# Where three scatters stand among GpSimd's gathers in a two-layer graph kernel on one core

## The chip, the cores and the metric

The kernel runs on one core of one Trainium2 chip. The metric is the device time of one execution in microseconds (us); smaller is better. A core has TensorE (PE in the profile), VectorE (DVE), ScalarE (ACT), GpSimd (POOL) and SyncE (SP), which run side by side, and 16 DMA engines that all of them feed. Each engine takes its own instructions strictly in program order: an instruction that waits holds up everything behind it on that engine. GpSimd issues here the DMAs whose row numbers are data: gathers (rows of a DRAM tensor into an SBUF tile) and scatters (rows of an SBUF tile into a DRAM tensor). The instruction on GpSimd ends when the transfer is issued; the data land later.

## The reference, cut to what matters

x has 2708 rows of 512 floats, adj is 2708 x 2708, with about 0.3% of its places filled.

```python
rowsum = adj.sum(axis=1)
d = where(rowsum > 0, rowsum ** -0.5, 0)
z = ((d[:, None] * adj * d[None, :]) @ x) @ W + b
h = layernorm(x + relu(z))                            # layer 0
xn = h @ W_node + b_node
feats = einsum('nd,hdf->hnf', xn, K)                  # 4 heads
s = leaky_relu(feats . A_self + feats . A_neigh)
attn = softmax(s[:, :, None] - 1e10 * (1 - adj))      # over the neighbours j
out = layernorm(h + relu(mean over heads of attn @ feats))   # layer 1
```

In layer 1 the term that is multiplied by 1e10 decides the softmax: a row gives all its weight to the neighbour with the largest adj value (s is the same for all j of a row). So layer 1 is a gather. With u = h @ M + c, where M and c join W_node, b_node and the mean of K, row i of the result is layernorm(h[i] + relu(u[top(i)])).

## The kernel before, in words

Rows go in blocks of 128: 21 full blocks (NS = 21) and one of 20 rows. A preparation finds the entries of each adj row and makes v = d * (x @ W), which goes to DRAM as v_d. **Layer 0** is a loop over the 21 blocks and, in each, over 9 chunks (C = 9); a step is n = 9 * block + chunk. A chunk is one gather of 128 rows of v_d on GpSimd (`fetch`, L650) and one product that adds them up (a matmul, L713, or an operation on VectorE, L703). Rows that do not fit this scheme, the last 20 among them, are "listed": at most 128 rows that are computed densely as an extra block L = 21.

When a block's sum is complete, `norm_1` (L754 and L755) and the steps behind it make h. A table `agenda` holds what is to be done at which step; `after(n, b, args)` enters the steps of block b: centre (L768), root, normalise, turn h (L244), `u_product` (L255) and `u_store` (L861 makes the tile ut from the product, then it is stored). The rows of u go to two DRAM tensors: u_e for the first 18 blocks (EARLY = 18) and u_d for blocks 18, 19 and 20. Blocks 0 to 16 are stored in plain order by SyncE; blocks 17 to 20 and the listed rows by scatters on GpSimd (`put`, L1198), because rows that are listed have to be left out.

**Layer 1.** For each block n a gather `y_fetch(n)` (L1221, called y0 to y20 here) takes the rows u[top(i)] out of u_e into a buffer. Rows whose neighbour lies in u_d are outside the bounds and left alone; they are late rows. `y_1` adds and sums (L1232 on VectorE, then the mean at L773, and the squares on ScalarE, L774), `root_1` and `root_2` make the scale for a group of blocks, `y_3` normalises (L805 on ScalarE or L810 on VectorE), and `out_store` (L1245, SyncE) stores a group. These steps are cut into 34 pieces; piece k holds y_fetch(k) and y_1(k-6). From step 173 to 185 of layer 0, ten pieces are run beside the last two blocks (three steps in four). What is left is run after the loop.

The late rows are packed into four tiles of 128 (NLATE = 4), numbers L+1 to L+4, beside the listed tile L. Each of the four needs its rows of h (`late_h`, a gather from h_d, L650) and its rows of u (a gather from u_d with the index top_d). Tile L has two gathers into one and the same buffer: from u_e with the index top_l (called yL here), and from u_d with top_d; so the second waits until the first has landed. The order of the gathers from u_d is L+1, L+2, L, L+3, L+4 (L1465), and all of them follow every scatter into u_d. Then come y_1, roots and y_3 of the five tiles (L1484 to L1500, in the groups L+1, L+2, L and L+3, L+4), and five scatters into the output (`rows_out`, L1476), which also have to follow the plain stores of the output.

All these buffers come from `row_space` (L656), a ring over two pools of 12 tiles: a tile's space is used again by the 24th request after it.

In the code before, the scatter of block 18 (S18 here) stands at step 180, that of block 19 (S19) at L1445, and that of block 20 (S20) at L1459, all inside `u_store` at L869.

Of the kernel before, what the change touches and what calls it, by code (L numbers as in the profile page):

```python
# [47 lines left out]
P = 128  # L48
# [5 lines left out]
EARLY = 18  # L54
NLATE = 4
# [8 lines left out]
def tile_two_graph_layers(  # L64
# [12 lines left out]
    N, D = x.shape  # L77
# [7 lines left out]
    NS = N // P  # L85
    GROUPS = [0, 4, 12, NB]

    def rows(ib):
        return min(P, N - ib * P)
# [15 lines left out]
    def many(dram_t, lo, hi):  # L105

        return dram_t[lo * P : hi * P, :].rearrange("(n p) d -> p n d", p=P)
# [12 lines left out]
    u_e = dram.tile([EARLY * P, D], F32, name="u_e")  # L120
    u_d = dram.tile([N - EARLY * P, D], F32, name="u_d")
# [534 lines left out]
    def row_space():  # L656

        ring[0] += 1
        if late is not None and ring[0] % 2:
            return late.tile([P, D], F32, name="g2", bufs=12)  # L660
        return g_pool.tile([P, D], F32, name="g", bufs=12)
# [100 lines left out]
    def centred(n, pr, t, junk):  # L762

        s = slice(n, n + 1)
        if n < ROOTS_AT:
            spread(n, pr, t, junk)
        else:
            nc.scalar.activation(junk[:pr], t[:pr], AF.Square, bias=nms[:pr, s], accum_out=sqs[:pr, s])  # L768
# [14 lines left out]
    def norm_2(lo, hi):  # L783

        s = slice(lo, hi)
        nc.gpsimd.tensor_tensor(rss[:, s], sqs[:, s], half_neg[:, : hi - lo], op=ALU.pow)

    def root_1(lo, hi):

        s = slice(lo, hi)  # L790
        nc.scalar.activation(sds[:, s], sqs[:, s], AF.Sqrt, scale=1.0 / D, bias=eps_1)
        nc.vector.tensor_scalar(vrs[:, s], sqs[:, s], 1.0 / D, EPS, op0=ALU.mult, op1=ALU.add)

    def root_2(lo, hi):

        s = slice(lo, hi)
        nc.vector.reciprocal(rss[:, s], sds[:, s])
        nc.vector.tensor_mul(vrs[:, s], vrs[:, s], rss[:, s])
        nc.vector.scalar_tensor_tensor(vrs[:, s], vrs[:, s], -0.5, rss[:, s], op0=ALU.mult, op1=ALU.mult)
        nc.vector.scalar_tensor_tensor(rss[:, s], vrs[:, s], 1.5, rss[:, s], op0=ALU.add, op1=ALU.mult)  # L800
        if hi - lo > 1:
            nc.vector.tensor_mul(nbs[:, s], nms[:, s], rss[:, s])
# [22 lines left out]
    def store_h(done):  # L825

        if done in H_ENDS:
            lo = ([0] + H_ENDS)[H_ENDS.index(done)]
            nc.sync.dma_start(out=many(h_d, lo, done), in_=h_part(lo, done))
# [3 lines left out]
    def turn_h(ib):  # L833
        hTs[ib] = turn(space(ib), P if ib == L else rows(ib), nc.scalar.copy)
# [3 lines left out]
    def u_product(ib):  # L838
        pr = P if ib == L else rows(ib)
        on_pe = searching[0]  # L840
        products_u[ib] = times(hTs.pop(ib), pr, m_sb, c_3 if on_pe else None), on_pe
# [3 lines left out]
    def u_store(ib):  # L845

        pr = P if ib == L else rows(ib)
        if ib == L:
            ut = dl["u"]
        else:  # L850
            if ib >= EARLY - 1:
                ut = row_space()
            else:
                if not ib % 2:
                    u_pair[:] = [pool2.tile([P, 2, D], F32, name="ut", bufs=1)]
                ut = u_pair[0][:, ib % 2, :]
        po, on_pe = products_u.pop(ib)
        if on_pe:
            nc.scalar.copy(ut[:pr], po[:pr])
        else:  # L860
            nc.vector.tensor_add(ut[:pr], po[:pr], c_bc[:pr])  # L861
        if ib < EARLY - 1:
            if ib % 2 or ib == EARLY - 2:
                lo = ib - ib % 2
                nc.sync.dma_start(out=many(u_e, lo, ib + 1), in_=u_pair[0][:, : ib + 1 - lo])
        elif ib == EARLY - 1:
            put(ut, u_e[:, :], dl["own"][:, ib : ib + 1], EARLY * P)
        elif ib != L:
            put(ut, u_d[:, :], dl["own_d"][:, ib : ib + 1], N - EARLY * P)  # L869


    L = NS
    dl = {}
# [7 lines left out]
    def at(n, f):  # L881
        agenda.setdefault(n, []).append(f)
# [314 lines left out]
    def put(t, dst, rows_at, n=N):  # L1197
        nc.gpsimd.indirect_dma_start(  # L1198
            out=dst,
            out_offset=bass.IndirectOffsetOnAxis(ap=rows_at, axis=0),  # L1200
            in_=t,
            in_offset=None,
            bounds_check=n - 1,
            oob_is_err=False,
        )


    ys = {}
    y_fetched = set()

    def y_fetch(n):

        if n in y_fetched:
            return
        y_fetched.add(n)
        ys[n] = row_space()
        fetch_some(ys[n], idx[:, n : n + 1], u_e[:, :], EARLY * P)

    def fetch_some(t, at, src, n):

        nc.gpsimd.indirect_dma_start(  # L1221
            out=t,
            out_offset=None,
            in_=src,
            in_offset=bass.IndirectOffsetOnAxis(ap=at, axis=0),
            bounds_check=n - 1,
            oob_is_err=False,
        )
# [30 lines left out]
    def pieces_y(k):  # L1259
        for _ in range(k):  # L1260
            for f in early_y.pop(0) if early_y else ():
                f()

    def y_ahead(k):

        nexts = [n for n in range(NS) if n not in y_fetched][:k]
        for n in nexts:
            y_fetch(n)

    def late_h(k):  # L1270
        h_of[L + 1 + k] = row_space()
        fetch(h_of[L + 1 + k], P, dl["read"][:, k : k + 1], h_d[:, :])
# [4 lines left out]
    C = len(CHUNKS)  # L1277
# [57 lines left out]
    def normed(b):  # L1335
        k = slice(b, b + 1)
        nc.scalar.activation(nbs[:, k], nms[:, k], AF.Copy, scale=rss[:, k])  # L1337
        norm_3(b, P, space(b))
        store_h(b + 1)

    def after(n, b, args):

        e = max(0, min(7, 15 - b))
        s = -1 if b == EARLY - 1 else 0
        at(n + 1 + s + min(2, e), lambda: centred(*args))
        if b >= ROOTS_AT:
            at(n + 2 + s + min(3, e), lambda: root_1(b, b + 1))
        at(n + 3 + s + min(4, e), lambda: norm_2(b, b + 1) if b < ROOTS_AT else root_2(b, b + 1))
        at(n + 3 + s + min(6, e), lambda: normed(b))
        if b < NS - 1:  # L1350
            at(n + 5 + s + e, lambda: turn_h(b))
            at(n + 7 + s + e, lambda: u_product(b))
        if b < NS - 2:
            at(n + 9 + s + e, lambda: u_store(b))

    def after_listed(n):
        at(n + 2, listed_norm)
        at(n + 3, lambda: root_1(L, L + 1))
        at(n + 5, lambda: root_2(L, L + 1))
        at(n + 5, lambda: norm_v(L, P, h_of[L]))  # L1360
        at(n + 6, lambda: turn_h(L))
        at(n + 8, lambda: u_product(L))
        at(n + 10, lambda: u_store(L))
# [6 lines left out]
    for ib in range(NS):  # L1370
        pr = rows(ib)
        for c in range(C):
            n = ib * C + c
# [60 lines left out]
        if ib < NS - 1:  # L1434
            after(n + 1, ib, args)
# [4 lines left out]
    ib = NS - 1  # L1440
    centred(*args)
    for n in sorted(agenda):
        for f in agenda.pop(n):
            f()
    u_store(ib - 1)  # L1445
    y_ahead(3)
    root_1(ib, ib + 1)
    pieces_y(1)
    root_2(ib, ib + 1)
# [3 lines left out]
    turn_h(ib)  # L1453
    pieces_y(1)
    u_product(ib)
    y_ahead(4)
    pieces_y(3)
    y_ahead(NS)
    u_store(ib)  # L1459
    for k in range(NLATE):  # L1460
        late_h(k)
    ys[L] = row_space()
    fetch_some(ys[L], dl["top"][:, NLATE:], u_e[:, :], EARLY * P)

    order = [L + 1, L + 2, L] + list(range(L + 3, L + 1 + NLATE))  # L1465
    for n in order:
# [180 lines left out]
```

## Time and profile before

| | us |
|---|---|
| median of 5 runs | 504.63 |
| the five runs | 504.63, 507.56, 501.21, 501.43, 506.9 |
| the profiled execution | 502.18 |
| its span, first to last instruction | 500.5 |

| engine | busy, us | share of the span |
|---|---|---|
| PE | 383.3 | 77% |
| DVE | 370.5 | 74% |
| ACT | 318.9 | 64% |
| POOL | 299.1 | 60% |

A row of the timeline gives the start in us from the start of the span, the length in us, the engine, the line of the kernel (L...), the operation, output <- inputs, and in square brackets how long the engine had been idle and what released it. "issue" means that it waited for nothing that the profile shows. A row of the view of waits gives the engine and line that waited, what it waited for, the total in us, how often, and the longest. A row of the view by stretches gives the busy time of PE, PEld (weight load), DVE, ACT and POOL with the number of instructions, the granted clock, the DMA engines' share and GB/s.

### The profile page before, as it was taken

The page shows a single profiled execution, that of the slowest core. Times are in us where ns is not written, and L with a number is a line of the kernel's source. Part 1 is how long each engine was busy: PE and PEld are TensorE (multiplying, and loading weights), DVE is VectorE, ACT ScalarE, POOL GpSimd, SP SyncE. Part 2 cuts the span into 40 slices and gives each one's busy share as a digit, 9 for nine tenths or more (in the row PEclk, how much of TensorE's full clock was granted, in tenths as well). Part 3 has the DMA queues.
Part 4 walks back from the last instruction along what each step waited for, and adds up shares of the span by engine and source line. Part 5 has one row for each costly group of instructions (what it writes and reads, how often), then busy time and mean ns, then how long its engine had stood idle before and what let it go on. Part 6 is the DMA issues. An engine that isn't in the chain of part 4 may idle for free. (4 is left out here: it accounts for less than half of the span.)

```text
span 500.5 us, 5439 instructions
## 1 busy us (share of the span) xinstructions
PE 383.3 (77%) x1299; PEld 176.5 (35%) x1299; DVE 370.5 (74%) x1058; ACT 318.9 (64%) x592; POOL 299.1 (60%) x423
## 2 busy tenths in 40 slices
PE   4978776869959999999867999959997768792000
PEld 3433333434214433333433444524442333351000
DVE  3699989699598899999597689744665375548751
ACT  1699999797972777879764764725662121337851
POOL 2333643453577677777787778776555627647624
PEclk8999999998998999999896999998999799988555
DMA  7999999997578587887999989997959635548972
GB/s 233 424 395 420 402 341 369 372 331 277 179 231 318 171 272 215 295 295 225 303 304 344 346 299 316 371 411 242 333 159 361 183 96 174 191 121 254 313 274 81
DMA packets 50251, 140.66 MB, mean 281 GB/s; under 512 B 9305, under 2 KB 9305, under 8 KB 47376
## 3 DMA queue, kind: packets, MB, share of 16 engines
q0 software_dynamic: 21696, 68.29, 42.8%
q1 hardware_dynamic: 28516, 71.95, 38.6%
q8 instruction: 12, 0.20, 0.2%
q14 instruction: 27, 0.22, 0.1%
HBM read 117.33 MB, written 24.99 MB: 284 GB/s over the span
## 5 line engine op out<-in xcount | busy, mean ns | idle before, releaser
L650 POOL DMA_INDIRECT g<-v_d,l_col x126 | 127.8, 1015 | 61.3 <-issue 30.7
L713 PE MATMUL acc<-g,s 128*128 128x512 f32 x272 | 140.6, 637 | 5.5 <-DMA g<-v_d,l_col 3.4
L255 PE MATMUL acc<-w_sb,sT 128*128 128x512 f32 (+1 forms) x176 | 84.7, 626 | 0.0
L255 PE MATMUL po<-m_sb,sT 128*128 128x512 f32 x176 | 82.8, 615 | 0.7 <-ACT sT L246 0.7
L650 POOL DMA_INDIRECT g<-v_d,cols x63 | 64.8, 1029 | 21.4 <-issue 11.7
L336 DVE MAX8 vals<-a 128x8 f32<-128x896 f32 (+2 forms) x66 | 71.7, 1086 | 4.1 <-ACT a L314 4.1
L337 DVE FIND_INDEX8 ats<-vals,a 128x8 uint32<-128x896 f32 (+2 forms) x66 | 72.0, 1091 | 0.0
L713 PEld LDWEIGHTS acc<-g,s 128*128 128x128 f32 x272 | 49.8, 199 | 53.6 <-issue 45.9
L314 ACT ACTIVATE a<-a 128x2708 f32<-128x2708 f32 (+1 forms) x22 | 54.6, 2480 | 10.5 <-POOL a L329 10.4
L321 ACT ACTIVATE a<-a 128x2708 f32<-128x2708 f32 (+1 forms) x22 | 54.1, 2461 | 3.4 <-DVE ats L337 3.4
L255 PEld LDWEIGHTS po<-m_sb,sT 128*128 128x128 f32 x176 | 34.8, 201 | 45.6 <-issue 40.7
L690 ACT ACTIVATE s<-s,l_val,l_minus 128x128 f32<-128x128 f32 x92 | 45.3, 493 | 3.1
L255 PEld LDWEIGHTS acc<-w_sb,sT 128*128 128x128 f32 (+1 forms) x176 | 33.2, 199 | 35.6 <-issue 35.6
L329 POOL TENSOR_SCALAR_AFFINE_SELECT a<-a 128x128 f32<-128x128 f32 (+1 forms) x22 | 6.3, 286 | 64.7 <-DMA a<-in_adj_dram 63.0
L246 ACT COPY sT<-tp 128x512 f32<-128x512 f32 (+1 forms) x44 | 25.5, 580 | 27.9 <-PE tp L244 27.8
L754 DVE TENSOR_TENSOR vs<-acc,vs 128x512 f32<-128x512 f32 x20 | 13.7, 687 | 35.5 <-PE acc L713 34.5
L703 DVE SCALAR_TENSOR_TENSOR vs<-g,scaled,vs 128x512 f32<-128x512 f32 x53 | 39.4, 744 | 0.5 <-DMA g<-v_d,l_col 0.4
L244 PE MATMUL tp<-ident,x 128*128 128x128 f32 (+1 forms) x88 | 15.0, 297 | 27.8 <-DMA x<-in_x_dram 17.1
L689 ACT ACTIVATE s<-place,l_row 128x128 f32<-128x128 f32 x92 | 35.7, 388 | 0.2 <-PE acc L713 0.2
L1337 ACT ACTIVATE nbs<-nms,rss 128x1 f32<-128x1 f32 x20 | 5.9, 293 | 46.8 <-DVE rss L800 30.2
L768 ACT ACTIVATE xr<-h_late,nms 128x512 f32<-128x512 f32 x13 | 9.3, 715 | 33.0 <-DVE nms L759 33.0
L1221 POOL DMA_INDIRECT g<-u_e,idx x21 | 22.2, 1056 | 7.4 <-issue 4.6
(284 smaller groups left out, 581.4 us busy)
## 6 DMA issues: line engine op xcount, KB each, us to landing
a<-in_adj_dram SPq DMA_DIRECT2D x21, 1354.0 KB, 18.1
x<-in_x_dram SPq DMA_DIRECT2D x21, 256.0 KB, 7.9
l_v<-v_d SPq DMA_DIRECT2D x7, 768.0 KB, 6.4
vs<-v_d SPq DMA_DIRECT2D x10, 512.0 KB, 10.9
xr<-in_x_dram SPq DMA_DIRECT2D x10, 512.0 KB, 9.7
u_e<-ut SPq DMA_DIRECT2D x8, 512.0 KB, 4.9
h_early<-in_L_gnn_K_dram POOLq DMA_DIRECT2D x3, 1024.0 KB, 19.2
v_d<-vs POOLq DMA_DIRECT2D x5, 512.0 KB, 9.8
```

Source lines behind the costliest of these rows:

```text
L246: copy(sT[:, :, :pr], ps[:, :, :pr])
L255: nc.tensor.matmul(po[:pr], sT[:, f, :pr], wt[:, f, :], start=(f == 0 and row_3 is None), stop=(f == ND - 1))
L314: nc.scalar.activation(blocks_a[ib][:pr], blocks_a[ib][:pr], AF.Copy, accum_out=sums[:pr, ib : ib + 1])
L321: nc.scalar.activation(blocks_a[ib][:pr], blocks_a[ib][:pr], AF.Relu, scale=-1.0, accum_out=bad[:pr, NB + ib : NB + ib + 1])
L336: nc.vector.max(out=vals[:pr, ib, t, :], in_=part)
L337: nc.vector.max_index(out=ats[:pr, ib, t, :], in_max=vals[:pr, ib, t, :], in_values=part)
L650: nc.gpsimd.indirect_dma_start(out=t[:pr], out_offset=None, in_=src, in_offset=bass.IndirectOffsetOnAxis(ap=ap, axis=0))
L689: nc.scalar.activation(s[:, :pr], place[:, :pr], AF.Abs, bias=minus_row[:, t : t + 1])
L690: nc.scalar.activation(s[:, :pr], s[:, :pr], AF.Relu, scale=minus_val[:, t : t + 1], bias=val[:, t : t + 1])
L703: nc.vector.scalar_tensor_tensor(vs, g, scaled[:, ib, CHUNKS[c][1], 0:1], vs, op0=ALU.mult, op1=ALU.add)
L713: nc.tensor.matmul(acc[ib][:pr], ss.pop((ib, c))[:k, :pr], g[:k], start=(first and not bias_on_pe(ib)), stop=(c == len(CHUNKS) - 1),)
L1221: nc.gpsimd.indirect_dma_start(out=t, out_offset=None, in_=src, in_offset=bass.IndirectOffsetOnAxis(ap=at, axis=0), bounds_check=n - 1, oo ...
```

## The change

`u_store` no longer scatters blocks 18 to 20; it makes the tile and returns it, and a new function `put_late` scatters it at another place. S18 moves from step 180 to step 188, the loop's last, S19 from ahead of the gathers that follow the loop to behind four of them, and S20 to behind yL, which moves from behind the four gathers of `late_h` to ahead of S20. No instruction is added or taken away; what is computed is the same.

```diff
@@ u_store
         elif ib != L:
-            put(ut, u_d[:, :], dl["own_d"][:, ib : ib + 1], N - EARLY * P)
+            return ut
@@ after
+    kept = []
...
-        if b < NS - 2:
+        if b < EARLY:
             at(n + 9 + s + e, lambda: u_store(b))
+        elif b < NS - 2:
+            at(n + 9, lambda: kept.append((b, u_store(b))))
+            at(NS * C - 1, lambda: put_late(*kept.pop(0)))
+
+    def put_late(ib, ut):
+        put(ut, u_d[:, :], dl["own_d"][:, ib : ib + 1], N - EARLY * P)
@@ behind the loop
-    u_store(ib - 1)
-    y_ahead(3)
+    kept.append((ib - 1, u_store(ib - 1)))
+    y_ahead(4)
+    put_late(*kept.pop())
     root_1(ib, ib + 1)
     pieces_y(1)
...
     u_product(ib)
-    y_ahead(4)
     pieces_y(3)
     y_ahead(NS)
-    u_store(ib)
+    ys[L] = row_space()
+    fetch_some(ys[L], dl["top"][:, NLATE:], u_e[:, :], EARLY * P)
+    put_late(ib, u_store(ib))
     for k in range(NLATE):
         late_h(k)
-    ys[L] = row_space()
-    fetch_some(ys[L], dl["top"][:, NLATE:], u_e[:, :], EARLY * P)
```

## The prediction

> **What bounds the kernel now.** I read the page first. No engine is busy through the span (PE 77%, DVE 74%), and the chain of work that ended last names one instruction of the program's end, so it carries nothing. The change touches only what GpSimd does behind step 180, so I read the timeline from 425 us on, GpSimd first:
>
> ```profile
> 430.56 1.01 POOL L1221 DMA_INDIRECT g<-u_e,idx  x1 [0.30 <-issue]
> 433.84 1.21 POOL L1198 DMA_INDIRECT u_d<-g,own_d  x1 [2.28 <-DVE g L861]
> ...
> 440.85 1.00 POOL L1221 DMA_INDIRECT g<-u_e,idx  x1 [0.31 <-issue]
> 447.44 1.01 POOL L1198 DMA_INDIRECT u_d<-g,own_d  x1 [5.59 <-DVE g L861]
> ...
> 462.59 1.00 POOL L1221 DMA_INDIRECT g<-u_e,idx  x1 [0.30 <-ACT h_early L805]
> 463.89 1.02 POOL L1198 DMA_INDIRECT u_d<-g,own_d  x1 [0.30 <-DVE vrs L799]
> 465.22 1.22 POOL L650 DMA_INDIRECT g<-h_d,to_read  x1 [0.31 <-issue]
> ...
> 470.50 1.00 POOL L1221 DMA_INDIRECT g<-u_e,top_l  x1 [0.30 <-ACT h_late L805]
> 471.81 1.00 POOL L1221 DMA_INDIRECT g<-u_d,top_d  x1 [0.31 <-issue]
> 473.11 1.00 POOL L1221 DMA_INDIRECT g<-u_d,top_d  x1 [0.30 <-ACT g L774]
> 477.76 0.99 POOL L1221 DMA_INDIRECT g<-u_d,top_d  x1 [3.65 <-DMA g<-u_e,top_l]
> ...
> 480.35 1.00 POOL L1221 DMA_INDIRECT g<-u_d,top_d  x1 [0.30 <-issue]
> 488.21 1.01 POOL L1198 DMA_INDIRECT out_dram<-g,to_put  x1 [6.86 <-ACT g L805]
> ```
>
> S18, S19 and S20 are the three rows u_d<-g,own_d. In front of S18 and S19 GpSimd stands still for 2.28 and 5.59 us, because ut is not made yet (DVE L861), with gathers behind it that need nothing of it. In front of S20 there is no wait: it is its place behind y20 that makes it late. And at 477.76 the second gather of tile L stands 3.65 us until yL, issued at 470.50, has landed in the same buffer. Then the waits of VectorE and the rows of VectorE and ScalarE in the same stretch:
>
> ```profile
> DVE vs L754 <- PE acc L713: 10.8, 2, 5.7
> DVE rss L797 <- ACT sds L791: 4.7, 8, 0.9
> DVE l_h L1232 <- DMA g<-u_d,top_d: 3.5, 1, 3.5
> ```
> ```profile
> 476.96 1.52 ACT L805 ACTIVATE h_late<-h_late,nbs,rss 128x512 f32<-128x512 f32 x2 [0.32 <-DVE nbs L802]
> 478.23 0.69 DVE L1232 SCALAR_TENSOR_TENSOR g<-g,g 128x512 f32<-128x512 f32 x1 [0.84 <-DMA g<-u_d,top_d]
> 479.04 0.74 DVE L1232 SCALAR_TENSOR_TENSOR g<-g,g 128x512 f32<-128x512 f32 x1
> 483.48 0.69 DVE L1232 SCALAR_TENSOR_TENSOR l_h<-g,l_h 128x512 f32<-128x512 f32 x1 [3.51 <-DMA g<-u_d,top_d]
> 484.40 0.72 ACT L774 ACTIVATE g<-l_h,nms 128x512 f32<-128x512 f32 x1 [3.58 <-DVE nms L773]
> 485.25 0.30 ACT L791 ACTIVATE sds<-sqs,eps 128x3 f32<-128x3 f32 x1
> ```
> ```profile
> 464.00:478.50 14.50, 0.19 (x2) 0.11 (x2) 10.50 (x46) 12.88 (x27) 8.72 (x9) 0.50 0.93 324
> 478.50:488.20 9.70, 0.00 (x0) 0.00 (x0) 5.00 (x22) 4.64 (x11) 2.24 (x3) 0.50 0.63 242
> ```
>
> No gather y0 to y20 appears among VectorE's waits: the blocks' layer 1 is paced by ScalarE and VectorE in turn (ScalarE busy 12.88 of 14.50 us) and is over at 478.48. From there the end hangs on DMA: VectorE waits 0.84 us for L+1's rows and 3.51 us for L's, issued at 477.76 and used at 483.48 (5.72 us). The roots of the first three tiles need L's squares (end 485.22), the output scatters need the roots, and from 488.21 on all is fixed: five scatters, then 12.3 us to the end.
>
> **The change part by part.** Counted from the loop (a piece at steps 173, 175, 176, 177, 179, 180, 181, 183, 184 and 185), S18 comes to stand behind 10 gathers, S19 behind 14, S20 behind 22 with yL; before, the trace shows 5, 10 and 21. One gather more or less ahead of S18 or S19 would be 1.3 us on GpSimd and change nothing below.
>
> A gather costs GpSimd 1.06 us (mean of the 21 y) and 0.30 us of issue: 1.36 us; a scatter 1.3, a late_h 1.31 (mean 1.01 and 0.30).
>
> *S18.* y5 starts at 431.9 in place of 435.36, since y4 ends at 431.57. Five gathers take 6.8 us, to 438.7; S18, whose tile is made at 433.56, goes there until 440.0. The wait of 2.28 us is gone. The buffers of y5 to y9 were those of block 19's chunks 1 to 5, all multiplied before 430.6 (block 19's sum is read at 430.69), so no wait takes its place.
>
> *S19.* y10 to y13 run from 440.0 to 445.4; their buffers are those of chunks that ended by 433. S19 still waits for its tile (L861 at 446.48 plus 0.68), so it starts at 447.44 as now, its wait about 2 us. Behind it stand y14 to y20, seven in place of eleven: 448.75 to 458.3 (7 x 1.36). y20's buffer is that of block 20's last chunk, read by 444.94.
>
> *yL and S20.* yL goes 458.3 to 459.6 in place of 470.50. S20, its tile made at 455.74 and so no wait, goes to 460.9, 1.7 us sooner than now (463.89 to 459.6) in spite of the gather put ahead of it. Four late_h run to 466.1; the last store of h_d was issued at 449.65, 11 us ahead of them. Then L+1 at 466.1, L+2 at 467.4, L at 468.7, L+3 at 470.0 and L+4 at 471.3. yL needs 7.0 us from its start (470.50 to 477.46); it has landed at 465.3, 3.4 us before L wants its buffer. S20's landing (3.2 us) is over at 462.8.
>
> *What it is worth.* With 5.7 to 7.0 us of landing, L+1 is there by 473.1, L by 475.7, L+4 by 478.3. They are asked for at 477.4 and later, when VectorE has done the last L810 (476.84 + 0.54). So the end goes by engines: L1232 of the three at 477.39, 478.20 and 479.01 (pitch 0.81), the means ready at 478.27, 479.08 and 479.89 (0.88 from a start, as at 478.23 to 479.11), ScalarE free at 478.48, the three squares of 0.87 us (0.72 and 0.19 overlapping) at 478.48, 479.37 and 480.25, the last over at 481.12 in place of 485.22. What follows keeps its order and lengths: a gain of 4.1 us, first output scatter at 484.1. Nothing else on PE, VectorE or ScalarE is moved. Alone, the swap of yL with S20 gives most of it: without the earlier y's, L would go at 474.4 and land at 480.1 in place of 483.48, 3.4 us. The moves of S18 and S19 give the last 0.7 and the reserve.
>
> *DMA.* y5 to y13 move into 431 to 447, where the DMA engines are 53% busy (425 to 447.5), out of a stretch with 71%; the rest moves ahead of 478, out of the stretch with the output stores. I take nothing for it. Bounds: below, the output scatters must follow the last plain store, issued at 478.50; transfers ceased at 485.0 in this execution, so if that stays the scatter goes at 485.0 in place of 488.21 and the gain is 3.2. I take 4.1, since three gathers of 256 KB (0.77 MB, 1.9 us at the 400 GB/s of those microseconds) leave the stretch. Above, 4.4 us is all that ScalarE idles (0.67, 0.14 and 3.58) in this execution.
>
> The Trainium skill (DMA: Bandwidth & Descriptors, Anatomy of one DMA) puts a DMA from GpSimd at about 2.0 us plus its bytes at 436 GB/s, an estimate of 2.6 us for 256 KB. By it yL would have landed at 474.1, there would be almost no wait at 477.76 and the change would be worth under 1 us; the trace shows 7.0 and 5.7 us, and the measurement decides.
>
> The sum: 500.5 - 4.1 = 496.4 us of span; the execution's own time 502.18 - 4.1 = 498.1. The median of the five runs lies 2.45 us over this execution, so from it the sum is 500.5. Two runs lie near 501.3, three at 504.6 to 507.6, so I do not know which kind will be in the middle and take the mean of both, 499.3.
>
> **The rivals.**
>
> *More.* The wait removed is a chain of two landings, 7.0 and 5.7 us. In an execution whose landings are 20% longer the chain grows by 2.5 us and the removed wait with it: 6.6 us, 495.6 from the profiled execution and 498.0 from the median. For it: three runs are 2.4 to 5.4 us over the profiled one, and something made them so. Against: they may as well be longer elsewhere.
>
> *Little or nothing.* The output stores, or a landing that gets longer in the crowded 458 to 472, take the place of the removed wait: if L+4 or L lands after 479 the gain sinks by as much, and with the stores at 485.0 it is 3.2 or, were they 2 us later for the gathers now ahead of them, 1: 503.6 from the median. Against: reserves of 3 us and more at every gather.
>
> *Slower.* The fetches of GpSimd that move into 431 to 447 run beside the chain of block 20 on VectorE, on which the whole end hangs. If a GpSimd instruction held up a VectorE operation while it runs, four gathers more (y10 to y13) at 1.0 us would cost up to 4.0 us there, and five moved ones (y5 to y9) another 5: from 4.1 us on it decides, and the full 9 would give 504.63 + 4.9 = 509.5. Against it: L754 takes 0.69 us at 430.69 beside a gather and 0.69 at 444.94 beside none, and 21 L1232 take 676 to 691 ns whether or not GpSimd is busy.
>
> The Trainium skill (SBUF — State Buffer, SBUF: two separate sides) has this as a rule: a VectorE operation with two SBUF inputs and a GpSimd operation that reads SBUF take a shared port as an exclusive lock. By that rule the 9 us are the worst case; the rows just named show no such wait.
>
> **How the numbers follow.** Gain of 3.2 to 5: 0.55. More: 0.20. Little or nothing: 0.17. Slower: 0.08. The likeliest gives 499.3; its own range is 497.2 (502.18 - 5) to 501.4 (504.63 - 3.2). The range reaches from 495.6, the rival with more, to 504.0, most of the rival with little. A measurement of this kernel can tell about 1%, 5.0 us, from no change. Faster by more than that: all of the second case and a quarter of the first, whose 4.1 us lie just under the bound: 0.34. Slower: 0.06 out of the last case. Within: 0.60.
>
> **What would show it.** Right: 10 gathers ahead of S18 and no wait there; S19 still released by L861 near 447.4 with 2 us; yL near 458 and S20 near 460; the five gathers from u_d without a gap, near 466 to 471; no wait of L1232 for DMA; the first output scatter near 484. Wrong: a wait at L1232 for top_d as before, an output scatter released by a store's DMA, L754 of block 20 later than 444.9, or a wait of GpSimd for a buffer among y5 to y13.

## The result, and the profile after

| | us |
|---|---|
| median before, 94 runs | 503.81 |
| median after, 52 runs | 501.21 |
| after / before | 0.9939, 95% interval 0.9922 to 0.9956 |
| the profiled execution after | 503.63 |
| its span | 501.9 |

The ratio is taken over the fast executions of both kernels alone, so it is not the quotient of the two medians, which lie 2.6 us apart. By the ratio the change is worth 0.61% (3.1 us; 2.2 to 3.9 by the interval), clear of noise. The median of 501.21 us lies inside the forecast's range (495.6 to 504.0), and the gain inside the 1% within which the forecast put it with a chance of 0.60. The gain is below the 4.1 us of the forecast's sum and just under the 3.2 us with which its likeliest case began.

The profiled span is 1.4 us longer than before's, and that is no contradiction: the last block's sum (L754) was read at 449.38 in this execution and at 444.94 in the one before. In the ten traces of the experiments below it lay between 444.02 and 450.82, and as widely in the kernels that leave S18 and S19 in their place (444.02 to 449.86) as in those that move them (444.05 to 450.82). The change does move gathers and S18 ahead of this sum, but from block 19's L754 to block 20's passed 14.25 us before and 14.24 after, and 14.2 to 14.3 in every trace. So the shift is not the change's, and every stage below is counted from the start of L754 of block 20, written L754 + so many us.

The timeline of GpSimd after:

```profile
439.04 1.36 POOL L1221 DMA_INDIRECT g<-u_e,idx  x1 [0.31 <-DVE vrs L792]
440.70 1.40 POOL L1198 DMA_INDIRECT u_d<-g,own_d  x1 [0.30 <-DVE rss L800]
...
446.62 1.00 POOL L1221 DMA_INDIRECT g<-u_e,idx  x1 [0.30 <-issue]
451.87 1.01 POOL L1198 DMA_INDIRECT u_d<-g,own_d  x1 [4.25 <-DVE g L861]
...
462.65 1.00 POOL L1221 DMA_INDIRECT g<-u_e,top_l  x1 [0.30 <-issue]
463.96 1.38 POOL L1198 DMA_INDIRECT u_d<-g,own_d  x1 [0.30 <-DVE nms L773]
...
471.22 1.01 POOL L1221 DMA_INDIRECT g<-u_d,top_d  x1 [0.30 <-issue]
...
473.85 1.00 POOL L1221 DMA_INDIRECT g<-u_d,top_d  x1 [0.30 <-issue]
...
489.93 1.01 POOL L1198 DMA_INDIRECT out_dram<-g,to_put  x1 [11.98 <-ACT sds L791]
```

Ten gathers stand ahead of S18, 14 ahead of S19, 22 ahead of S20. The 2.28 us in front of S18 and the 3.65 us in front of tile L's second gather are gone, and that gather goes at L754 + 24.5 in place of + 32.8. In front of S19 GpSimd still stands 4.25 us. VectorE's waits from 425 us on, and the rows of the late tiles:

```profile
DVE vs L754 <- PE acc L713: 12.4, 2, 6.7
DVE rss L797 <- ACT sds L791: 4.8, 8, 0.9
DVE vrs L792 <- ACT g L774: 2.4, 4, 1.0
DVE vrs L792 <- ACT xr L768: 0.3, 1, 0.3
```
```profile
481.48 1.52 ACT L805 ACTIVATE h_late<-h_late,nbs,rss 128x512 f32<-128x512 f32 x2 [0.32 <-DVE nbs L802]
481.81 0.68 DVE L1232 SCALAR_TENSOR_TENSOR g<-g 128x512 f32<-128x512 f32 x1
483.43 0.68 DVE L1232 SCALAR_TENSOR_TENSOR l_h<-g,l_h 128x512 f32<-128x512 f32 x1
484.34 0.72 ACT L774 ACTIVATE g<-l_h,nms 128x512 f32<-128x512 f32 x1
485.19 0.30 ACT L791 ACTIVATE sds<-sqs,eps 128x3 f32<-128x3 f32 x1
487.06 1.52 ACT L805 ACTIVATE g<-g,nbs,rss 128x512 f32<-128x512 f32 x2
```

The first view is complete, and no DMA is among these waits: L1232 for tile L no longer waits its 3.51 us. The root of the three tiles (sds, 3 columns) comes at L754 + 35.81 in place of + 40.31, a gain of 4.5 us. But the first norm is done at 487.86 (487.06 and 0.80 for one of the two) and the first output scatter starts only at 489.93, L754 + 40.55 in place of + 43.27. Only 2.7 us of the 4.5 arrive. The releaser named, sds L791, is the second root at 489.31, for tiles that this scatter does not touch; a wait for several semaphores is put down to the latest one that the profile knows. What SyncE and the DMA engines did just then:

```profile
483.02 0.37 SPq L1245 DMA_DIRECT2D out_dram<-h_late  x1
```
```profile
482.50:487.50 5.00, 0.00 (x0) 0.00 (x0) 3.84 (x19) 4.21 (x11) 0.00 (x0) 0.50 0.96 362
487.50:489.60 2.10, 0.00 (x0) 0.00 (x0) 0.91 (x4) 2.07 (x5) 0.00 (x0) 0.50 0.03 12
```

The last plain store of the output is issued at 483.02; the DMA engines are 96% busy until 487.5, and a trickle (3%) follows. Before, the same store was issued at 478.50, transfers ceased at 485.0, and the scatter came 3.2 us after that, released by ScalarE's norm. So theory A: the moves take away the wait for tile L's gather, and then the last output store, late because the DMA engines are full, holds the scatter. Rival B: something else holds it, or nothing does and the gap is chance.

### The profile page after: what moved, and what is told of

Read it like the earlier page. It is cut to its first block, busy times and chain, and to the rows that moved or that the text cites. A ratio compares the mean times of both kernels' runs of the same rounds, so it can differ in the third digit from the quotient of the medians.

```text
span 501.9 us, 5441 instructions
## 1 busy us (share of the span) xinstructions
PE 386.9 (77%) x1299; PEld 177.4 (35%) x1299; DVE 369.8 (74%) x1058; ACT 318.5 (63%) x592; POOL 301.9 (60%) x423
## 5 line engine op out<-in xcount | busy, mean ns | idle before, releaser
L255 PE MATMUL po<-m_sb,sT 128*128 128x512 f32 x176 | 84.4, 625 | 0.7 <-ACT sT L246 0.7
L754 DVE TENSOR_TENSOR vs<-acc,vs 128x512 f32<-128x512 f32 x20 | 13.7, 687 | 39.8 <-PE acc L713 38.6
```

The lines of the kernel that those rows point to most:

```text
L255: nc.tensor.matmul(po[:pr], sT[:, f, :pr], wt[:, f, :], start=(f == 0 and row_3 is None), stop=(f == ND - 1))
```

## The experiments

All ratios are against the kernel before on the same chip. The stages are in us after L754 of block 20, each from one trace. "First scatter" is the start of the first output scatter; "last packet" is the end of the last one that the DMA engines moved ahead of it, read in slices of 0.04 us. Where no ratio stands, there were too few runs for one.

| kernel | root of three tiles | last packet | first scatter | ratio to before, interval |
|---|---|---|---|---|
| before | 40.31 | 40.0 | 43.27 | |
| the change, first trace | 35.81 | 39.1 | 40.55 | 0.9939 (0.9922 to 0.9956) |
| the change again | 35.81 | 38.4 | 39.80 | 0.9945 (0.9912 to 0.9979) |
| the swap alone | 37.86 | 41.1 | 42.48 | 0.9972 (0.9935 to 1.0008) |
| S18 and S19 alone | 35.80 | 37.8 | 39.29 | 0.9946 (0.9916 to 0.9977) |
| all gathers ahead of S19 | 35.81 | 39.0 | 40.39 | 0.9937 (0.9903 to 0.9972) |
| the same, S19 into its own tensor | 35.88 | 37.5 | 39.03 | |
| the change, last store aside | 35.88 | 38.8 | 38.91 | |
| before, last store aside | 40.12 | 40.5 | 43.36 | 1.0006 (0.9968 to 1.0044) |
| the change, last store twice | 35.80 | 40.3 | 41.74 | 0.9968 (0.9934 to 1.0002) |
| the swap alone, last store aside | 37.52 | 40.7 | 40.89 | 0.9950 (0.9913 to 0.9988) |
| seven gathers ahead of S19 | 35.81 | 37.5 | 38.98 | 0.9920 (0.9884 to 0.9956) |

**The change again.** No edit.

> The changed kernel once more, on the chip of the next three. Stage measured from the start of block 20's L754 to the first output scatter: 40.55 us as in its first trace (before: 43.27). Both theories: 2.7 to 3.1 us faster than before.

Measured: a ratio of 0.9945, and the first scatter at 39.80. The root is at the same 35.81 to the hundredth, the scatter 0.75 us sooner and the last packet 0.7: what follows the root varies from execution to execution, as a landing would.

**The swap alone.** On the kernel before:

```diff
+    ys[L] = row_space()
+    fetch_some(ys[L], dl["top"][:, NLATE:], u_e[:, :], EARLY * P)
     u_store(ib)
     for k in range(NLATE):
         late_h(k)
-    ys[L] = row_space()
-    fetch_some(ys[L], dl["top"][:, NLATE:], u_e[:, :], EARLY * P)
```

> The kernel before with yL ahead of S20 alone; S18 and S19 stand where they stood. Theory A (the gain is the wait of tile L's second gather; then the output stores hold the first output scatter): the three squares end 3.4 us earlier, the first output scatter comes 41.0 us after L754 (2.3 us earlier than before) and is held by the stores. Rival B (no store holds it, only the chain of landings counts): 39.9 us, 3.4 us faster. Rival C (S18 and S19 bring the gain): no change.

```profile
484.34 0.69 DVE L1232 SCALAR_TENSOR_TENSOR g<-g 128x512 f32<-128x512 f32 x1 [1.83 <-DMA g<-u_d,top_d]
```
```profile
476.88 1.01 POOL L1221 DMA_INDIRECT g<-u_d,top_d  x1 [0.30 <-issue]
...
492.34 1.01 POOL L1198 DMA_INDIRECT out_dram<-g,to_put  x1 [8.95 <-ACT sds L791]
```

A miss for every theory. L's own wait went, as expected, but the first late tile, L+1, is now the late one: its gather at 476.88 is read at 484.34, 7.5 us later, where 6.4 us passed before (471.81 to 478.23). The root gains 2.45 us and not 3.4, and 1.7 us of that is held back at the scatter. The time is 0.28% shorter, with an interval that includes no change. At the scatter, 0.8 us sooner, Rival C came nearest.

**S18 and S19 alone.** On the changed kernel, yL put back behind `late_h`:

```diff
-    ys[L] = row_space()
-    fetch_some(ys[L], dl["top"][:, NLATE:], u_e[:, :], EARLY * P)
     put_late(ib, u_store(ib))
     for k in range(NLATE):
         late_h(k)
+    ys[L] = row_space()
+    fetch_some(ys[L], dl["top"][:, NLATE:], u_e[:, :], EARLY * P)
```

> S18 and S19 moved as in the change, yL left behind the four late_h. Theory A: GpSimd gets there 5 us sooner, so L's second gather, although it still waits for yL, lands before VectorE asks for it; no wait of L1232 for DMA, the first output scatter 40.6 to 41.3 us after L754, 2.0 to 2.7 us faster. The opposite theory, that only the swap takes the wait away: no change, with 3 us of wait at L1232 left.

```profile
465.10 1.45 POOL L1221 DMA_INDIRECT g<-u_e,top_l  x1 [0.30 <-issue]
...
472.13 1.39 POOL L1221 DMA_INDIRECT g<-u_d,top_d  x1 [2.97 <-DMA g<-u_e,top_l]
...
484.24 1.01 POOL L1198 DMA_INDIRECT out_dram<-g,to_put  x1 [8.13 <-ACT g L805]
```

The wait for yL is still there, 2.97 us at 472.13, and it costs nothing: it ends at L754 + 27.2, early enough for the gather behind it. The root is where the whole change has it, and so is the time, 0.9946 against 0.9945. S18 and S19 bring all of the gain that can be measured; yL's swap adds nothing to them that these intervals show. The scatter, at 39.29, comes earlier than the 40.6 to 41.3 expected, and earlier than in either trace of the whole change, although the gathers from u_d go later here (to L754 + 30.2 in place of + 27.1). What made it earlier, the order or the spread from execution to execution, these traces do not tell apart.

**All gathers ahead of S19.** On the changed kernel:

```diff
-    y_ahead(4)
+    y_ahead(NS)
+    ys[L] = row_space()
+    fetch_some(ys[L], dl["top"][:, NLATE:], u_e[:, :], EARLY * P)
     put_late(*kept.pop())
...
-    y_ahead(NS)
-    ys[L] = row_space()
-    fetch_some(ys[L], dl["top"][:, NLATE:], u_e[:, :], EARLY * P)
     put_late(ib, u_store(ib))
```

> The changed kernel with all of y10 to y20 and yL ahead of S19. GpSimd's wait of 4.25 us in front of S19 is filled, and all later gathers are issued about 4 us sooner, so their bytes are gone when the output stores come. Theory A (the stores are held up by the gathers' bytes, and hold up the scatter): first output scatter 38.8 us after L754, 1.7 us ahead of the changed kernel, 4.5 us (0.9%) faster than before. Rival B (something else than the stores holds the scatter): 40.5 us, as the changed kernel.

```profile
462.63 1.25 POOL L1198 DMA_INDIRECT u_d<-g,own_d  x1 [0.30 <-DVE nms L773]
468.87 1.01 POOL L1198 DMA_INDIRECT u_d<-g,own_d  x1 [4.98 <-DVE nms L773]
...
475.84 1.46 POOL L1221 DMA_INDIRECT g<-u_d,top_d  x1 [0.30 <-issue]
```

A miss, and one that says nothing on A and B: the wait taken away in front of S19 came back, 4.98 us, in front of S20, and the gathers from u_d start at L754 + 25.0, later than in the change (+ 21.8). Their 3.2 us of delay cost nothing at the root (35.81). S20 seemed to wait for S19 to land in the same tensor.

**The same, with S19 into a tensor of its own** (the late rows miss block 19's rows of u):

```diff
+    u_x = dram.tile([N - EARLY * P, D], F32, name="u_x")
...
     def put_late(ib, ut):
-        put(ut, u_d[:, :], dl["own_d"][:, ib : ib + 1], N - EARLY * P)
+        dst = u_x if ib == NS - 2 else u_d
+        put(ut, dst[:, :], dl["own_d"][:, ib : ib + 1], N - EARLY * P)
```

> All gathers ahead of S19, as before, but S19 goes into a DRAM tensor of its own, so the late rows miss block 19's rows of u. If the wait of 4.98 us in front of S20 (S20 18.05 us after L754, S19 at 11.81) is S20 waiting for S19 to land in the same tensor, it goes: S20 at about 13.1 us, the gathers from u_d at 20 to 26 us in place of 25.0 to 30.7, the first output scatter at 38.8 to 39.8 in place of 40.4. If S20 waits for something on VectorE or ScalarE, as the profile's name for it says (DVE nms L773), it stays at 18 us.

```profile
455.86 1.25 POOL L1199 DMA_INDIRECT u_x<-g,own_d  x1 [0.30 <-DVE nms L774]
457.41 1.01 POOL L1199 DMA_INDIRECT u_d<-g,own_d  x1 [0.30 <-DVE vrs L800]
```

The wait is gone, S20 goes at L754 + 13.36, the gathers from u_d at 20.3 to 25.9, the first scatter at 39.03. So it was S19's landing, not the VectorE operation that the profile names. (One execution of this kernel was taken.)

**The last output store aside.** On the changed kernel; the rows of blocks 19 and 20 go to a tensor of their own, with the same bytes at the same place:

```diff
+    o_d = dram.tile([N // P * P, D], F32, name="o_d")
...
-        nc.sync.dma_start(out=many(out, lo, hi), in_=h_part(lo, hi))
+        nc.sync.dma_start(out=many(o_d if hi == NS else out, lo, hi), in_=h_part(lo, hi))
```

> The changed kernel, but the plain store of blocks 19 and 20 goes to a DRAM tensor of its own, so these rows of the output are left out; the same bytes move at the same place, and the first output scatter has only to wait for the store before it (blocks 16 to 18). Theory A: the scatter starts 38.8 to 39.3 us after L754 of block 20, 1.3 to 1.8 us sooner than in the changed kernel. Rival B (no store holds it): 40.5 us.

```profile
489.36 1.01 POOL L1199 DMA_INDIRECT out_dram<-g,to_put  x1 [10.84 <-ACT g L806]
```

At L754 + 38.91, released by ScalarE's norm and 0.36 us after it (+ 38.55): A, not B. This rests on the trace; the six times of this kernel (493.65 to 503.95) spread too far to add to it. The same on **the kernel before**:

> The same taken from the kernel before: the store of blocks 19 and 20 goes aside, these rows are left out. Both theories: no change, 43.3 us from L754, since there ScalarE released the scatter, not a store. If it gets faster, the wait for the store was there already before the change.

43.36 against 43.27, ratio 1.0006: before, the store held nothing. And on **the swap alone**:

> The swap of yL and S20 alone, and the store of blocks 19 and 20 aside (these rows of the output are left out). In the trace of the swap alone the first late tile is normed 40.5 us after L754 and the first output scatter starts at 42.5. Theory A (a store holds it): 40.8 to 41.2 us, 1.3 to 1.7 us sooner than with the swap alone. If the swap alone is slow for another reason: 42.5 us.

40.89 in place of 42.48, as A expects; with the store out of the way the swap is worth 0.50%, though its interval overlaps that of the swap alone.

The table's last packets say the same. In the eight traces in which the late rows come sooner than before and the store stays in the output, the first scatter starts 1.4 to 1.5 us after the last packet (0.30 us of GpSimd's issue included), wherever that lies between 37.5 and 41.1; with the store aside it starts 0.2 us after it, and in the two of the kernel before, where ScalarE is later, 2.9 and 3.3 us.

**The last output store twice.** On the changed kernel:

```diff
     def out_store(lo, hi):
+        if hi == NS:
+            nc.sync.dma_start(out=many(o_d, lo, hi), in_=h_part(lo, hi))
         nc.sync.dma_start(out=many(out, lo, hi), in_=h_part(lo, hi))
```

> The changed kernel with one more store of blocks 19 and 20 (512 KB), to a DRAM tensor of its own, just ahead of the last store of the output. Theory A: 512 KB at about 395 GB/s are 1.3 us, the first output scatter comes 41.9 us after L754, 1.3 us slower than the changed kernel. Rival B: 40.5 us, no slower.

```profile
492.18 1.01 POOL L1199 DMA_INDIRECT out_dram<-g,to_put  x1 [13.19 <-issue]
```

41.74, as A had it (41.9); the root stays at 35.80. Another 512 KB ahead of the last store delay the scatter by 1.2 us against one trace of the change and 1.9 against the other. The time, 0.9968, lies between the change and no change, and its interval reaches both.

**Seven gathers ahead of S19.** What the failure of "all gathers" taught: leave S19 where its tile is just made, fill the wait in front of it, and keep S20 well behind it.

```diff
-    y_ahead(4)
+    y_ahead(7)
     put_late(*kept.pop())
```

> The changed kernel with seven gathers (y10 to y16) ahead of S19 in place of four; yL and S20 as in the change. GpSimd's wait in front of S19 (4.25 and 1.64 us in the two traces of the change) is filled, S19 stays at 2.5 us after L754 of block 20, S20 moves from 14.6 to about 11 us, far enough behind S19 to find it landed, and the gathers from u_d from 21.8-27.1 to about 18-23.5 us. Theory A (the last output stores are late because the gathers' bytes are still under way): first output scatter 38.8 to 39.4 us after L754, 0.4 to 1.7 us ahead of the change, 3.9 to 4.5 us faster than before. Rival (the stores' own 2.3 MB make them late): 39.8 to 40.6 us, as the change.

```profile
446.87 1.01 POOL L1198 DMA_INDIRECT u_d<-g,own_d  x1 [0.30 <-issue]
...
455.41 1.28 POOL L1198 DMA_INDIRECT u_d<-g,own_d  x1 [0.92 <-DVE vrs L792]
...
462.93 1.01 POOL L1221 DMA_INDIRECT g<-u_d,top_d  x1 [0.30 <-issue]
...
483.26 1.01 POOL L1198 DMA_INDIRECT out_dram<-g,to_put  x1 [13.62 <-ACT g L805]
```

The gathers from u_d go at L754 + 18.65 to 24.4 and the scatter at 38.98. The profile puts it down to ScalarE's norm, yet it stands 1.5 us behind the last packet as in the other traces. The stretch of the last stores, L754 + 30 to + 38.6, in the change and in this kernel:

```profile
479.40:488.00 8.60, 0.19 (x2) 0.11 (x2) 6.60 (x29) 7.48 (x17) 0.00 (x0) 0.50 0.93 352
```
```profile
474.30:482.90 8.60, 0.19 (x2) 0.11 (x2) 6.60 (x29) 7.49 (x17) 0.00 (x0) 0.50 0.74 274
```

The engines' work is the same to 0.01 us; the DMA engines are 74% busy where they were 93%, since the gathers' bytes, and those of the stores before, are gone by then: 274 GB/s over 8.60 us are 2.36 MB, just the 2304 KB of the three stores issued in this stretch, where the change moved 3.03 MB. The scatter stands 0.49 us behind the norm, where 2.07 and 1.3 us passed in the change and 0.3 to 0.4 where no store holds it. How much of this the three gathers more ahead of S19 bring is not shown: S18 and S19 alone came to 39.29 without them. Ratio 0.9920, 4.0 us: the lowest ratio here, but its interval overlaps the change's (0.9939).

## Why the prediction was right, and where it was wrong

*Place and direction: right.* The time is in GpSimd's order, and no VectorE wait for a gather is left. S18 went at once, S19 was still released by L861 at L754 + 2.5, the gathers from u_d had no gap, and no wait for a buffer came up among y5 to y13. S19's wait was 4.25 us in one trace and 1.64 in the other, where 2 were forecast. Two of the listed signs of being wrong showed all the same: L754 came later than 444.9, which the change did not cause, and a store held the output scatter, which is the step that failed below.

*"A gain of 4.1 us, first output scatter at 484.1": the first half nearly right, the second wrong.* The root gained 4.5 us; the 0.4 too little (it even passes the 4.4 us set as the upper bound) is the pitch of the three squares, taken as 0.87 to 0.89 us and measured as 0.71 and 0.73 (482.90, 483.61, 484.34). But "what follows keeps its order and lengths" failed: between norm and scatter stood 2.07 us in the first trace and 1.3 in the second, in place of 0.3. The gain at the scatter was 2.7 and 3.5 us in the two traces, and the times give 3.1. One reading was wrong besides: S20 at 459.6 in place of 463.89 is 4.3 us sooner and not 1.7; measured from L754 it came 4.4 us sooner (+ 14.58 in place of + 18.95). Nothing in the sum hangs on it.

*"DMA. I take nothing for it": the step that failed.* The right mechanism was named as the lower bound, the output scatter behind the last plain store, but sized too kindly: the end of the transfers (485.0) was taken for the landing. After the change, the bulk ended at 487.5, single transfers went on until 488.4, and the scatter started at 489.93. With the 1.4 to 1.5 us that stand between the last packet and the scatter wherever the store holds it, 485.0 would have meant 486.4 and a gain of 1.8 us, not 3.2. The last packet came 0.9 and 1.7 us sooner after L754 than before, and that makes the 2.7 and 3.5. The 0.77 MB taken off for three gathers was nearly the right amount for another reason: behind L754 + 33.6 the DMA engines moved 2.35 MB before and 1.66 MB after, but only 0.26 MB of the 2.35 were in the queue of GpSimd's DMAs (q0); the rest of the difference is stores that were further along. In the first trace part of what this won was lost again to the single transfers behind the bulk.

*"Alone, the swap of yL with S20 gives most of it": wrong.* I gave it 3.4 us and S18 and S19 0.7. Measured: 0.28% (1.4 us; interval from 3.3 us faster to 0.4 slower) against 0.54% (2.7 us). These two intervals overlap; the traces decide, with the root 2.5 us sooner by the swap and 4.5 us by S18 and S19. The swap takes yL's landing out of tile L's way, but leaves all five gathers as late as they were, in the crowd of the stores, where L+1 took 7.5 us in place of the 6.4 that I read before. Moving S18 and S19 starts all five sooner, and then yL's wait costs nothing. So it is in part luck that the total came near: the sum gave most of the gain to the move that adds nothing measurable to the other two, and a root 0.4 us better than forecast made up for part of the hold.

*The rivals.* "Little or nothing" named what took 1.0 to 1.8 us of the gain. "Slower", by GpSimd beside VectorE, did not show: L754 took 0.69 us again and L1232 0.68 to 0.69, and the step from block 19's sum to block 20's stayed at 14.2 us. "More", by longer landings, is not told apart from the run-to-run spread.

*The estimate of 2.6 us for a landing from the Trainium skill* (DMA: Bandwidth & Descriptors, Anatomy of one DMA) would have made the change worth under 1 us; the median landings of the gathers from u_d were 5.7 us before and 6.7 us after, and the change was worth 3.1.

## What to carry to other kernels

A scatter or store whose data come late belongs behind the gathers that need nothing of it, but keep it clear of the next write to the same tensor, which here waited until it had landed. When a wait at the end is taken away, list everything else that the last step waits for, with the time at which each is ready, and count a store as ready at its landing, not at the end of its bytes: here the first scatter came 1.4 to 1.5 us after the last packet. And a wait that is visible in a trace is worth something only if what is behind it is late: the 2.97 us in front of tile L's gather cost nothing once GpSimd was there 5 us sooner.

## What the hardware showed that was not expected

Landings of gathers of up to 128 rows (256 KB) ranged widely: 3.6 us (median of the 21 y after, where the DMA engines were 56% busy from 425 to 462.5 us) and 6.7 us (the five from u_d, where they were 99% busy from 471.4 to 479.4). A scatter that waited for a store started 1.4 to 1.5 us after the last packet, in eight traces. A scatter into a tensor delayed the next scatter into it by 5.9 us from its start (462.63 to 468.57, where S20's own issue of 0.30 us began). Twice the profile named an engine as releaser where the experiment showed a DMA: sds L791 for the output scatter, nms L773 for S20.
